# A four-layer image network on one core: VectorE takes the centered copy of the scan's first norm, and the variances' product is issued one chunk later

## The chip, the cores and the metric

The kernel runs on one core of one Trainium2 chip. The metric is the device time of one execution in microseconds (us). The engines named here are TensorE (PE in the profile; its weight loads are PEld), VectorE (DVE), ScalarE (ACT), GpSimd (POOL) and SyncE (SP), which issues most of the DMAs. TensorE writes its products to PSUM; ScalarE and VectorE read them from there.

## The reference

The input is eight images of 64 channels and 128 x 128 pixels, in fp32. Four layers follow each other, each of the form x + layer(groupnorm(x)): a deformable convolution, a 3 x 3 convolution, a pair of scans in two directions (an S5 block), and a layer of neighbours and upsampling. The change lies in the third, at the first layer norm over the 64 channels of a pixel:

```python
def _layer_norm(x, g, b):
    mu = jnp.mean(x, axis=-1, keepdims=True)
    var = jnp.mean((x - mu) ** 2, axis=-1, keepdims=True)
    return (x - mu) * jax.lax.rsqrt(var + EPS) * g + b
def _s5_block(x, i, ln1_g, ln1_b, ...):
    fx = _layer_norm(x, ln1_g[i], ln1_b[i])
    h = _s5_scan(fx, lam_re[i], lam_im[i], B_re[i], B_im[i], C_re[i], C_im[i], D[i], log_step[i])
    x = jax.nn.gelu(h) + fx
    ...
```

The x that enters here is a group-normalised one, and the mean over channels is the same for both scan directions, so the centered and scaled values are made once and used by both.

## The kernel before

Two images make a pair: 2 x 64 channels fill the 128 partitions, and a pair's 128 x 128 pixels lie along the free dimension. There are four pairs. The deformable layer runs first for all pairs (some 14,200 us); then, pair by pair, come the 3 x 3 convolution (`conv3x3`), the scans (`scan_layer`) and the last layer (`neighbours`), whose steps are partly laid into the next pair's convolution.

`scan_layer` begins with `first_norm`, which works through the 16,384 pixels of a pair in 32 chunks of 512 (`CH`), four to a block (index `n`, from the last block to the first; `m` counts the chunks in a block). For each chunk:

- L902: a product with the centering matrix, scaled by the group norm's factor, gives the centered values `pc` in PSUM. The PSUM tag "x" has two buffers, so the third centering reuses the buffer of the first.
- L904: ScalarE squares `pc` plus a bias column `cn` into `sq`. The tiles alternate between the tags "sq" and "xt", one buffer each.
- L905: ScalarE copies `pc` plus `cn` into `bf`, the room of the pair (in the profile: `room`).
- L906: `variances` (L855, the product on L858) multiplies a matrix of channel means with `sq`; the four chunks of a block write four strips of 32 partitions in one PSUM tile `pv` (in the profile: `l1v`).

After four chunks ScalarE copies `pv` to `vs` (L908, again in the buffer of tag "sq"). `by_pixel` (L860) transposes it (L865) and takes the reciprocal root on VectorE: fifteen small steps of `rsqrt` (L111 to L121). One block later `scale` (L890) spreads those roots over the channels: GpSimd copies them wide (L872), TensorE transposes them (L875), VectorE multiplies `bf` by them (L894).

`first_norm` is a generator. From its second block on, each block is followed by two steps of `back`, the backward scan of the first direction. A step of `back` holds `drive` (L1235 a product, ScalarE's copy `v` L1237, a second product L1238, two VectorE multiplications L1241 that read `pv` and `pt`, a GpSimd addition L1242), `inputs` (L1224: two ScalarE instructions that scale `bf`, each followed by two DMAs L1226 issued by SP), and `scan` (L1250 a small product, L1255 ScalarE's copy of it, L1257 two scans on VectorE, and a DMA of the result issued by SP, L1271). `inputs` reads what `scale` has multiplied, so the four L1224 of a block wait for the last L894 of that block.

The order of instructions on each engine is not the order of the source. The builder lays it out by priority (the earlier in the source, the higher) among what is ready in its own reckoning, then every engine runs its own list strictly in order, with semaphores for the dependences.

Of the kernel before, what the change touches and what calls it, by code (L numbers as in the profile page):

```python
# [11 lines left out]
AF = mybir.ActivationFunctionType  # L12
# [29 lines left out]
class Net:  # L42
# [835 lines left out]
    def first_norm(self, wp, p, a, b, r, nb):  # L878


        nc = self.nc
        af, bf = a.rearrange("p h w -> p (h w)"), b.rearrange("p h w -> p (h w)")
        center = wp.tile([P, P], F32, tag="center_r", name=f"center_r{p}", bufs=1)
        nc.vector.tensor_scalar(center, self.center, r, None, ALU.mult)
        pn = self.ps1.tile([P, 1], F32, tag="small", name=f"cn{p}")
        nc.tensor.matmul(pn, lhsT=self.center, rhs=nb, start=True, stop=True)
        cn = wp.tile([P, 1], F32, tag="cn", name=f"cns{p}", bufs=1)
        nc.vector.tensor_copy(cn, pn)

        def scale(n, y):  # L890
            for m in range(4):
                s = slice((4 * n + m) * CH, (4 * n + m + 1) * CH)
                rb = self.spread(wp, "y", y[:, 8 * m : 8 * m + 8], f"l1_{p}_{n}_{m}", ("ms0", "ms1")[m % 2])
                nc.vector.tensor_mul(bf[:, s], bf[:, s], rb)  # L894

        late = None
        for n in range(NCH // 4 - 1, -1, -1):
            pv = self.ps1.tile([P, CH], F32, tag="small", name=f"l1v{p}_{n}")
            for m in range(4):
                s = slice((4 * n + m) * CH, (4 * n + m + 1) * CH)  # L900
                pc = self.ps.tile([P, CH], F32, tag="x", name=f"pc{p}_{n}_{m}")
                nc.tensor.matmul(pc, lhsT=center, rhs=af[:, s], start=True, stop=True)  # L902
                sq = wp.tile([P, CH], F32, tag=("sq", "xt")[m % 2], name=f"sq{p}_{n}_{m}", bufs=1)
                nc.scalar.activation(sq, pc, AF.Square, bias=cn)  # L904
                nc.scalar.activation(bf[:, s], pc, AF.Identity, bias=cn)  # L905
                self.variances(pv, m, sq)  # L906
            vs = wp.tile([P, CH], F32, tag="sq", name=f"vs{p}_{n}", bufs=1)
            nc.scalar.copy(vs, pv)  # L908
            if late:
                scale(*late)  # L910
            y = self.by_pixel(vs, f"l1_{p}_{n}")
            if late:
                yield
            late = n, y
        scale(*late)
        yield
# [506 lines left out]
```

## Time and profile before

| What | Value |
|---|---|
| Timed runs of before, median | 18815.32 us (3 runs, 18770.06 to 18828.75) |
| Profiled execution, time | 18647.43 us |
| Profiled execution, span first to last instruction | 18645.6 us, mean granted TensorE clock 0.763 |
| Busy over the span | PE 11123.6, DVE 11377.5, ACT 3024.1, POOL 11000.0 us |
| L902 centering, L858 variances | 256 instructions each (two per product), median 595 and 617 ns |
| L904 square, L905 copy | 128 each, median 687 and 680 ns |
| L894 scaling | 128, median 681 ns |
| L1224 scan inputs, whole kernel | 512, mean 1292 ns |

[...] The busy time of TensorE depends on the clock it is granted, so the same instruction has short and long records. The profiled execution was 0.9% shorter than the median of the timed runs, so sums made from its rows are compared with its own span, not with the median.

In a line of the timeline stand the start and length in us, the engine, the line, the operation, the tile written and the tiles read, the count of merged instructions, and in brackets how long the engine had been idle before and who released it. In a line of waits stand the waiting instruction, the one it waited for, the us in total, the number of times and the longest. In a line of groups stand the busy us and mean ns, then the idle us ahead of the group and what ended it.

### The profile page before, as it was taken

The page shows a single profiled execution, that of the slowest core. Times are in us where ns is not written, and L with a number is a line of the kernel's source. Part 1 is how long each engine was busy: PE and PEld are TensorE (multiplying, and loading weights), DVE is VectorE, ACT ScalarE, POOL GpSimd, SP SyncE. Part 2 cuts the span into 40 slices and gives each one's busy share as a digit, 9 for nine tenths or more (in the row PEclk, how much of TensorE's full clock was granted, in tenths as well). Part 3 has the DMA queues.
Part 4 walks back from the last instruction along what each step waited for, and adds up shares of the span by engine and source line. Part 5 has one row for each costly group of instructions (what it writes and reads, how often), then busy time and mean ns, then how long its engine had stood idle before and what let it go on. Part 6 is the DMA issues. An engine that isn't in the chain of part 4 may idle for free. (4 is left out here: it accounts for less than half of the span.)

```text
span 18645.6 us, 118301 instructions
## 1 busy us (share of the span) xinstructions
PE 11123.6 (60%) x31224; PEld 3929.2 (21%) x31224; DVE 11377.5 (61%) x27180; ACT 3024.1 (16%) x5658; POOL 11000.0 (59%) x10484
## 2 busy tenths in 40 slices
PE   6655455545555554445654555555427988889886
PEld 1111111111111111111111111111102434435343
DVE  5566666556665556656665566555664765667566
ACT  1000111001100000010000000000003425334242
POOL 5766766666666666766666676766671413315142
PEclk8777677767777666777776777667658989999898
DMA  4333333333333333333333333333333243422423
GB/s 150 103 100 104 116 113 116 109 112 111 117 111 98 97 94 113 112 113 110 100 95 100 93 99 99 99 96 93 92 92 94 69 144 79 130 87 70 142 76 101
DMA packets 900049, 1933.33 MB, mean 104 GB/s; under 512 B 199852, under 2 KB 435764, under 8 KB 876340
## 3 DMA queue, kind: packets, MB, share of 16 engines
q0 software_dynamic: 442368, 1208.55, 21.7%
q1 hardware_dynamic: 381968, 679.49, 11.9%
q10 hardware_dynamic: 75044, 37.72, 1.0%
q8 instruction: 255, 4.18, 0.1%
q14 instruction: 414, 3.39, 0.1%
HBM read 1540.72 MB, written 208.10 MB: 94 GB/s over the span
## 5 line engine op out<-in xcount | busy, mean ns | idle before, releaser
L371 POOL DMA_INDIRECT g<-table,idx x9216 | 9526.3, 1034 | 4333.7 <-issue 2626.2
L381 DVE TENSOR_REDUCE sm<-g 128x64 f32<-128x256 f32 x9216 | 5062.9, 580 | 3356.0 <-remote 2479.9
L289 PE MATMUL po<-xe,wt 128*54 128x512 f32 (+3 forms) x8384 | 4668.4, 666 | 534.0 <-ACT ob L299 390.9
L380 DVE TENSOR_TENSOR g<-g,wts 128x256 f32<-128x256 f32 x9216 | 3561.8, 415 | 552.9 <-DMA g<-table,idx 488.5
L387 PE MATMUL sp<-ident,sm 128*128 128x128 f32 x4096 | 1494.5, 375 | 3632.2 <-DVE sm L381 1853.0
L390 ACT COPY s<-sp 128x512 f32<-128x512 f32 x1024 | 598.1, 584 | 9537.5 <-remote 3918.3
L387 PEld LDWEIGHTS sp<-ident,sm 128*128 128x128 f32 x4096 | 619.5, 155 | 6387.2 <-DVE sm L381 2381.4
L395 PE MATMUL yp<-s,wd 128*64 128x512 f32 (+1 forms) x2560 | 933.0, 736 | 1367.3 <-ACT s L390 756.3
L289 PEld LDWEIGHTS po<-xe,wt 128*54 128x54 f32 x8384 | 916.4, 138 | 1863.7 <-issue 1192.8
L872 POOL COPY l_yb<-ln_y 128x512 f32<-128x512 f32 x128 | 72.8, 612 | 1295.9 <-DVE ln_y L121 1295.9
L588 PE MATMUL c<-room,l_w 128*64 128x508 f32 (+1 forms) x3072 | 741.8, 597 | 22.2 <-DMA room<-nx 16.1
L1242 POOL TENSOR_TENSOR u<-u,v 128x512 f32<-128x512 f32 x256 | 327.9, 1281 | 680.0 <-DVE v L1241 548.8
L1224 ACT ACTIVATE fx<-room,ln_b,ln_g 128x512 f32<-128x512 f32 x512 | 639.2, 1292 | 169.9 <-DMA in<-fx 148.1
L1334 POOL TENSOR_TENSOR ms<-ms,ln_y 128x512 f32<-128x512 f32 x256 | 274.0, 1090 | 640.2 <-DVE ln_y L121 600.3
L389 PE MATMUL s<-ident,sm 128*64 128x128 f32 x1024 | 343.5, 335 | 449.7 <-DVE sm L381 151.2
L396 DVE BATCH_NORM_STATS2 ystat<-yp 128x6 f32<-128x512 f32 x128 | 89.3, 697 | 844.2 <-PE yp L395 498.7
L395 PEld LDWEIGHTS yp<-s,wd 128*64 128x64 f32 (+1 forms) x2560 | 222.9, 161 | 1810.2 <-issue 1000.3
L1257 DVE TENSOR_TENSOR_SCAN z<-tabs,z,u 128x256 f32<-128x256 f32 x512 | 435.4, 876 | 214.8 <-POOL u L1242 186.2
L1235 PE MATMUL pv<-in,tabs 128*128 128x512 f32 x1024 | 506.4, 617 | 41.9 <-DVE u L1241 40.0
L1320 PE MATMUL pc<-outs,h 128*128 128x256 f32 x2048 | 497.7, 386 | 28.0 <-DVE h L1305 25.8
L1302 PE MATMUL py<-x,outs 128*128 128x512 f32 x1024 | 507.3, 599 | 6.8 <-POOL x L1288 6.4
L1302 PE MATMUL py<-in,outs 128*128 128x512 f32 x1024 | 507.3, 608 | 1.7 <-ACT h L1304 1.0
(414 smaller groups left out, 10197.6 us busy)
## 6 DMA issues: line engine op xcount, KB each, us to landing
g<-table,idx POOLq DMA_INDIRECT x9216
in<-fx SPq DMA_DIRECT2D x1024, 128.0 KB
xe<-in_x_dram SPq DMA_DIRECT2D x56, 1408.0 KB
table<-q SPq DMA_DIRECT2D x256, 256.0 KB
y<-ys SPq DMA_DIRECT2D x128, 256.0 KB
room<-in_x_dram SPq DMA_DIRECT2D x64, 512.0 KB
yr<-y SPq DMA_DIRECT2D x64, 512.0 KB
room<-nx SPq DMA_DIRECT2D x256, 128.0 KB
```

What stands on the lines that cost most here:

```text
L289: nc.tensor.matmul(po[:, r0:r1, c0:c1], lhsT=wt[:, t, :], rhs=xe[:, row + r0 : row + r1, c0 + dx : c1 + dx], start=n == 0, stop=n == len(u ...
L371: nc.gpsimd.indirect_dma_start(out=tq[:, k, :], out_offset=None, in_=flat[i], in_offset=bass.IndirectOffsetOnAxis(ap=idx[:, at : at + 1], ...
L380: nc.vector.tensor_mul(t[:, k], t[:, k], w)
L381: nc.vector.tensor_reduce(sm[:, k], t[:, k].rearrange("p q c -> p c q"), axis=mybir.AxisListType.X, op=ALU.add)
L387: nc.tensor.transpose(sp[:, j, :], sm[:, j * P : (j + 1) * P], self.ident)
L390: nc.scalar.copy(st[i][:, 0:4, m * P : (m + 1) * P], sp)
L395: nc.tensor.matmul(yp[i * C : (i + 1) * C, :], lhsT=wd[0:rows, j, :], rhs=st[i][0:rows, j, :], start=j == 0, stop=j == 4)
L588: nc.tensor.matmul(o, lhsT=lt, rhs=mv, start=k < 2, stop=k >= len(calls) - 2)
L1224: nc.scalar.activation(fx[:, e].rearrange("p h (o m) -> p h o m", m=self.INNER), src[:, e::2], AF.Identity, bias=w["ln1_b"], scale=w["ln1_g"])
L1235: nc.tensor.matmul(pv, lhsT=tabs[:, at : at + P], rhs=fx[:, :, h, :], start=h == 0, stop=h == 1)
L1302: nc.tensor.matmul(py, lhsT=lt, rhs=mv, start=n == 0, stop=n == len(calls) - 1)
L1320: nc.tensor.matmul(pc[:, i], lhsT=hs[:, h, i, m * P : (m + 1) * P], rhs=self.outs[:, CEN : MIX + P], start=True, stop=True)
```

## The change

ScalarE no longer writes the centered values: VectorE does, with an addition of the same bias column out of the same PSUM tile. The variances' product of a chunk is issued after the centering, square and copy of the next chunk; the last chunk's product follows the loop. The number of instructions is the same: 128 ScalarE copies become 128 VectorE additions. No tile, buffer or DMA is added or removed.

```diff
                 nc.tensor.matmul(pc, lhsT=center, rhs=af[:, s], start=True, stop=True)
                 sq = wp.tile([P, CH], F32, tag=("sq", "xt")[m % 2], name=f"sq{p}_{n}_{m}", bufs=1)
                 nc.scalar.activation(sq, pc, AF.Square, bias=cn)
-                nc.scalar.activation(bf[:, s], pc, AF.Identity, bias=cn)
-                self.variances(pv, m, sq)
+                nc.vector.tensor_scalar_add(bf[:, s], pc, cn)
+                if m:
+                    self.variances(pv, m - 1, before)
+                before = sq
+            self.variances(pv, 3, before)
             vs = wp.tile([P, CH], F32, tag="sq", name=f"vs{p}_{n}", bufs=1)
             nc.scalar.copy(vs, pv)
             if late:
```

## The prediction

> **What bounds the kernel now.** I went from the whole to the place. By the page's 40 slices the last quarter of the span is the part after the sampling stage; the edited lines L902 to L906 run there and nowhere else: 128 chunks, 32 for each of four image pairs, in four stretches of about 145 us that begin at 14231, 15365, 16490 and 17620 us. Together they are some 575 us of 18645.6, 3.1%. I took the busy time of each engine in the first stretch, then in parts of one turn of its loop:
>
> ```profile
> 14231.00:14375.00 144.00, 123.83 (x352) 47.09 (x353) 62.48 (x176) 79.81 (x116) 28.97 (x39) 0.84 0.24 63
> ...
> 14319.98:14340.51 20.53, 17.84 (x52) 6.98 (x53) 10.03 (x28) 11.61 (x18) 4.82 (x6) 0.83 0.30 78
> 14318.31:14321.37 3.06, 0.36 (x3) 0.30 (x3) 2.70 (x8) 3.06 (x5) 0.22 (x1) 0.86 0.78 189
> 14321.37:14327.55 6.18, 6.18 (x7) 1.29 (x8) 1.99 (x9) 2.94 (x5) 2.27 (x4) 0.51 0.57 159
> 14327.55:14335.20 7.65, 7.65 (x31) 3.62 (x30) 3.08 (x5) 2.48 (x5) 1.27 (x1) 1.00 0.00 0
> ```
>
> The columns are the stretch, its length, then busy us of TensorE, its weight loads, VectorE, ScalarE, GpSimd, and the granted clock. A turn (four chunks, two scan steps) takes 20.53 us. TensorE has work for 17.84 of them, ScalarE for 11.61, VectorE for 10.03. TensorE stands nearly still for 3.06 us while ScalarE is full, and then works for 6.18 us at a clock of 0.51 before it comes back to 1.00. Its waits in that first stretch:
>
> ```profile
> PE l1v L858 <- ACT sq L904: 9.1, 7, 2.9
> PE pn L1250 <- DVE ln_t L120: 6.6, 4, 1.7
> ```
>
> The other three stretches give 9.0, 9.1, 9.0 and 6.6 each time: 36.2 and 26.4 us in all. The timeline shows what makes the square late:
>
> ```profile
> 14315.72 2.54 ACT L1224 ACTIVATE fx<-room,ln_b,ln_g 128x512 f32<-128x512 f32 x2 [0.52 <-DVE room L894]
> ...
> 14318.20 2.48 ACT L1224 ACTIVATE fx<-room,ln_b,ln_g 128x512 f32<-128x512 f32 x2
> ...
> 14319.98 0.35 PE L1250 MATMUL pn<-z,tabs 128*128 128x2 f32 x2 [1.67 <-DVE ln_t L120]
> ...
> 14320.62 0.70 ACT L904 ACTIVATE sq<-pc,cns 128x512 f32<-128x512 f32 x1
> ...
> 14321.20 0.69 ACT L905 ACTIVATE room<-pc,cns 128x512 f32<-128x512 f32 x1
> 14321.37 1.91 PE L858 MATMUL l1v<-sq,imgmean 128*32 128x512 f32 x2 [1.03 <-ACT sq L904]
> ...
> 14321.57 0.75 DVE L1257 TENSOR_TENSOR_SCAN z<-tabs,z,u 128x256 f32<-128x256 f32 x1
> ...
> 14323.21 2.08 PE L902 MATMUL pc<-room,center_r 128*128 128x512 f32 x2
> ...
> 14325.22 1.92 PE L858 MATMUL l1v<-sq,imgmean 128*32 128x512 f32 x2
> 14325.33 0.69 ACT L904 ACTIVATE sq<-pc,cns 128x512 f32<-128x512 f32 x1 [2.27 <-PE pc L902]
> ```
>
> So the loop closes thus: last multiplication of the late block (L894, ends 14315.68), four scan inputs L1224 on ScalarE (5.0 us), the first square, the variances' product, then TensorE without a gap until the next L894. The copy L905 stands behind the square: it is not in this loop. And TensorE already runs both centerings (L902, four instructions at 14316.35) before the first variances' product: the order that the second half of the edit asks for is there, although the source has it otherwise.
>
> **The change, part by part.**
>
> *ScalarE loses 128 copies.* L905 has a median of 0.680 us: 128 x 0.680 = 87 us of busy time go, 2.7 in a turn. After them ScalarE waits anyway (the third square waits 2.27 us for its product). The second square starts 0.57 us sooner (14321.20, not 14321.77), but its product comes after the third centering at 14325.22. On the path: 0.
>
> *VectorE gains 128 additions from PSUM.* This shape with this operation is not in the trace. Nearest are a copy out of PSUM with 512 columns and L1166, a scalar operation with a column of scalars out of PSUM, with 256 and 384 columns:
>
> ```profile
> L259 DVE COPY q<-tp 128x512 f32<-128x512 f32 x128 | 87.1, 680 | 12.4 <-PE tp L257 11.3 <-DMA table<-q 1.0
> ...
> L1166 DVE TENSOR_SCALAR d<-d,own 128x384 f32<-128x384 f32 x48 | 29.0, 605 | 0.0
> ...
> L1166 DVE TENSOR_SCALAR d<-d,own 128x256 f32<-128x256 f32 x16 | 7.5, 477 | 21.8 <-PE d L1163 21.8
> ```
>
> The slope of L1166 is (605 - 477) / 128 = 1.0 ns a column, so 733 ns at 512; the copy says 680. I take 0.70: 128 x 0.70 = 90 us, 2.8 in a turn, which lifts VectorE to 12.8 of 20.53. Chunks three and four fall into an idle stretch of 8.12 us (before L894 at 14331.64), which hides them. The first two fall among the scans and the small steps of the reciprocal root. That chain would end 1.4 us later, at 14325.3; GpSimd's four copies (2.27 us, now ended at 14326.0) would then end near 14327.4, and TensorE wants the first at 14330.95. Cover left: 3.5 us. Without it, each further us costs 28 us (seven closed turns in four pairs).
>
> *A new wait: the next centering for VectorE.* The third centering reuses the bank of the first, so it now waits for VectorE's copy. Are the two reads of one product side by side? The first use of pv, read by both engines, says no:
>
> ```profile
> 14266.55 0.59 ACT L1237 COPY v<-pv 128x512 f32<-128x512 f32 x1 [1.70 <-PE pv L1235]
> 14267.17 0.69 DVE L1241 TENSOR_TENSOR u<-pv,tabs 128x512 f32<-128x512 f32 x1 [9.81 <-ACT v L1237]
> ```
>
> VectorE idled 9.81 us until ScalarE's read of the same product had ended, and began 0.03 us after it. So the copy follows the square. The square ends at 14321.32, VectorE's second scan at 14322.32; copy until 14323.02 (0.70) or 14323.05 (0.73); with 0.05 us for the release the centering can start at 14323.1. It starts now at 14323.21, when TensorE is done with the slow variances' product. Cost: 0, or 0.1 us with one small step in front, 28 x 0.1 = 3 us. The upper end is a copy behind the whole reciprocal root chain (ends 14324.05): copy until 14324.75, centering at 14324.8, 1.6 us late, 28 x 1.6 = 45 us. The lower end is 0: nothing on the loop becomes shorter. I take 2 us. Behind the waiting copy stand small steps and the scale multiplications on VectorE; these have the 3.5 us above. No DMA is issued anew or moved past another.
>
> [...]
>
> *The product behind the next centering.* One product for each chunk either way, 0.85 to 1.0 us at full clock; in the first chunks of a pair, without scan steps, the trace goes by 2.03 us a chunk with TensorE unbroken (centering 14236.29, variances 14237.34, centering 14238.32). There the third centering's bank would be free at 14234.44 + 0.70 = 14235.14, before its 14236.29. Cost 0.
>
> Sum: -0 + 0 + 2 + 0 = 2 us. On the profiled execution (18647.43 us, span 18645.6) that gives 18649. That execution lies 0.9% under the median of the three timed runs, 18815.32; I carry the difference over and predict 18815, a change too small to be seen. A measurement of this kernel can tell about 0.3% from no change: faster is below 18759, slower above 18872.
>
> **Rivals.**
>
> *Faster: the order of the engines closes up.* What the builder lays out differs from the source, by when things are ready in its own reckoning, and with ScalarE lighter it could put a square before the scan inputs, or less work between the variances and the last L894. Then TensorE's waits go, 36.2 + 26.4 = 63 us (18752), and if it never stands still, the slow clock too: 6.18 x (1 - 0.51) = 3.03 us a turn, 28 x 3.03 = 85 us more (18667). Middle: 18710. For it: 2.7 us of idling in a turn are there to be had, and the clock row shows idling paid twice. Against it: all four inputs are ready when the first starts and are earlier in the source, and the edit touches none of them.
>
> [...]
>
> *Slower: VectorE holds the bank.* The additions stand behind the reciprocal root's steps in VectorE's order, the third centering comes 1.6 us late, and TensorE idles inside the stretch in which its clock should recover. Restarting the 6.18 us after the slow product of 1.84 us adds 1.84 x 0.49 = 0.9 us. Per turn 2.5, x 28 = 70 us: 18885. It decides as soon as the copy ends 0.15 us after 14323.05, and is past what can be told from 2.0 us a turn on. For it: the scans and the small steps fill 2.70 of 3.06 us just there. Against it: now the scans already slip in between these steps.
>
> *The edit does not do what it says*: reads follow each other, the order was there. That is part of my forecast, at the same time.
>
> **How the numbers follow.** No visible change 0.43: its working has bounds of 0 and 45 us, both inside 0.3%. Faster 0.28, slower 0.29: the order is laid out anew by a reckoning I cannot follow, and 2 us a turn suffice either way. Range 18690 to 18905: it holds the first case, most of the slower one and of the faster one down to three quarters of the way from 18759 to 18667; about 0.2 is left out.
>
> **What would show it.** Right: turns of about 20.5 us; L858 still waits some 36 us for squares; VectorE's additions of 0.68 to 0.73 us start as the squares end; ScalarE's busy time lower by 87 us. Wrong: L902 waiting for the new additions by over 1 us a turn and a longer slow-clock stretch (slower), or no wait of L858 and a clock near 1.00 in the stretches (faster). A squaring ahead of the scan inputs in ScalarE's order would make the prediction wrong at once.

## The result and the profile after

Twelve timed runs of the changed kernel have a median of 18818.11 us (18730.65 to 18856.55), twelve of the kernel before 18799.76 us (18726.26 to 18830.86). The ratio on record is 1.0004 with a 95% interval of 0.9989 to 1.0019 (the quotient of the two medians is 1.0010): no difference that can be measured, as forecast. The 2 us that the forecast's sum came to are far below what these runs can tell. The profiled execution has a span of 18780.6 us, 135 more than before's, but 124 of these lie ahead of the first norm (its first product starts at 14355.4, not 14231.2 us), in code that the change doesn't touch. So all that follows goes by the trace of the part concerned: the *four stretches* from L886, the first product of the first norm, to the first output product of the scan (L1302; lines after L905 are three higher in the changed kernel). They take 183.2, 174.6, 179.9 and 179.8 us before, in sum 717.5, and 179.3, 179.2, 184.0 and 179.4 us after, in sum 721.9: 4.4 us more.

The view of one line, for the new additions on VectorE in the kernel after:

```profile
L905 DVE TENSOR_SCALAR room<-pc,cns x128: 743/750/752, 14358.6 to 17886.6; 128x512 f32<-128x512 f32 x128
its engine sat idle before it (us, times) until:
  ACT sq L904: 106.7, 69
who waited for it (us, times):
  PEld pc L902: 12.9, 16
```

128 additions with a median of 0.750 us, and the idle times ahead of 69 of them ended with a square. Next the busy times of a settled turn (from a block's first variances' product, L858, to the next block's) and its parts, after, with the columns as in the prediction:

```profile
14442.47:14462.91 20.44, 16.71 (x53) 7.37 (x53) 13.62 (x32) 9.41 (x14) 4.86 (x6) 0.83 0.30 79
14438.75:14442.47 3.72, 0.00 (x1) 0.00 (x1) 2.49 (x7) 3.72 (x6) 0.93 (x1) 0.83 0.73 168
14442.47:14448.48 6.01, 6.01 (x11) 2.17 (x12) 3.01 (x10) 1.37 (x3) 2.27 (x4) 0.54 0.44 117
14448.48:14455.82 7.34, 7.34 (x33) 3.73 (x32) 4.82 (x8) 2.21 (x4) 1.28 (x1) 1.00 0.00 0
```

The turn is 20.44 us (20.53 before). ScalarE works 9.41 us in it (11.61 before), VectorE 13.62 (10.03). TensorE now stands still in one piece, for 3.72 us, and then works for 6.01 us at a granted clock of 0.54. The waits of TensorE in the first 146 us of the first stretch of the kernel after:

```profile
PE l1v L858 <- ACT sq L904: 23.0, 7, 5.1
PE cn L886 <- DVE gn_nb L149: 3.3, 1, 3.3
PE l_rb L875 <- DVE room L894: 0.4, 1, 0.4
```

The wait ahead of the small product (L1250 before, L1253 after) is gone from this list and the wait for squares has grown from 9.1 to 23.0 us (91.8 over the four stretches). The timeline of the kernel after shows why:

```profile
14436.88 4.91 ACT L1227 ACTIVATE fx<-room,ln_b,ln_g 128x512 f32<-128x512 f32 x4 [1.25 <-DVE room L894]
...
14441.68 0.15 ACT L1258 COPY z<-pn 128x2 f32<-128x2 f32 x1
14441.72 1.27 ACT L904 ACTIVATE sq<-pc,cns 128x512 f32<-128x512 f32 x2
...
14442.47 2.49 PE L858 MATMUL l1v<-sq,imgmean 128*32 128x512 f32 x4 [3.72 <-ACT sq L904]
```

The four scan inputs (L1227, L1224 before) still stand ahead of the squares, in one piece now, and the two squares follow each other without the copy between. TensorE makes both variances' products there before the third centering; before, it made one.

### The profile page after: what moved, and what is told of

It reads as the page before. It is cut to its first block, busy times and chain, and to the rows that moved or that the text cites. A ratio compares the mean times of both kernels' runs of the same rounds, so it can differ in the third digit from the quotient of the medians.

```text
span 18780.6 us, 118357 instructions
## 1 busy us (share of the span) xinstructions
PE 11000.9 (59%) x31224; PEld 3926.2 (21%) x31224; DVE 11460.3 (61%) x27308; ACT 2952.7 (16%) x5530; POOL 11065.3 (59%) x10484
## 5 line engine op out<-in xcount | busy, mean ns | idle before, releaser
L289 PE MATMUL po<-xe,wt 128*54 128x512 f32 (+3 forms) x8384 | 4593.3, 657 | 504.9 <-ACT ob L299 283.0
L588 PE MATMUL c<-room,l_w 128*64 128x508 f32 (+1 forms) x3072 | 739.3, 596 | 21.6 <-DMA room<-nx 15.2
L1227 ACT ACTIVATE fx<-room,ln_b,ln_g 128x512 f32<-128x512 f32 x512 | 638.9, 1291 | 200.2 <-DMA in<-fx 147.4
```

Of the source, the lines that this page charges most:

```text
L289: nc.tensor.matmul(po[:, r0:r1, c0:c1], lhsT=wt[:, t, :], rhs=xe[:, row + r0 : row + r1, c0 + dx : c1 + dx], start=n == 0, stop=n == len(u ...
L588: nc.tensor.matmul(o, lhsT=lt, rhs=mv, start=k < 2, stop=k >= len(calls) - 2)
L1227: nc.scalar.activation(fx[:, e].rearrange("p h (o m) -> p h o m", m=self.INNER), src[:, e::2], AF.Identity, bias=w["ln1_b"], scale=w["ln1_g"])
```

## The experiments

The runs were made on several chips (the record names 10, 12 and 13). The sampling stage doesn't take equally long in all runs (the first norm starts near 12,030 us in some and near 14,100 to 14,360 in others, both among those on chip 12), the part behind it hardly differs (e6 and e12, one program: 644.6 and 639.0 us over the four stretches), so the kernels are compared by their four stretches. "Turns" are from one copy L908 to the next, in the settled part of a stretch.

| Kernel | Four stretches, us | Sum |
|---|---|---|
| before | 183.2, 174.6, 179.9, 179.8 | 717.5 |
| before again (e13) | 182.0, 178.8, 173.8, 173.5 | 708.1 |
| after | 179.3, 179.2, 184.0, 179.4 | 721.9 |
| e1, VectorE's copy alone | 179.4, 179.3, 178.8, 175.6 | 713.1 |
| e2, new order alone | 183.4, 184.1, 183.6, 183.4 | 734.5 |
| e3, two squares on GpSimd | 172.0, 167.2, 171.2, 171.0 | 681.4 |
| e4, additions twice | 185.2, 186.5, 186.0, 184.8 | 742.5 |
| e5, inputs split, on after | 166.2, 167.3, 168.0, 168.0 | 669.5 |
| e6, inputs split, on before | 159.3, 162.9, 159.5, 162.9 | 644.6 |
| e8, e3 and e5 together | 164.5, 167.6, 162.6, 162.0 | 656.7 |
| e9, three useless products | 179.4, 179.6, 179.5, 179.6 | 718.1 |
| e10, two useless products | 171.5, 171.8, 173.1, 173.0 | 689.4 |
| e11, inputs split, on e2 | 164.6, 165.4, 164.9, 164.9 | 659.8 |
| e12, e6 timed | 159.3, 159.6, 160.9, 159.2 | 639.0 |

**The halves alone.** e1 takes only VectorE's copy:

```diff
-                nc.scalar.activation(bf[:, s], pc, AF.Identity, bias=cn)
+                nc.vector.tensor_scalar_add(bf[:, s], pc, cn)
                 self.variances(pv, m, sq)
```

> The kernel before with the first half of the change alone: VectorE writes the centered copy, the variances' product stays where it was in the source. Measure: the four stretches from the first-norm's first product to the first output product of the scan, summed (717.5 us before, 721.9 us with the whole change). Theory (the turn is closed by scan inputs, square, variances on ScalarE and TensorE; the copy is not in it): 712 to 728 us, a turn of 20.3 to 20.6 us. Rival (two parts that cancel: the copy gains or loses, the order gives it back): this stretch sum moves by over 15 us in one direction, and by as much the other way with the order alone.

e2 takes only the later product:

```diff
                 nc.scalar.activation(bf[:, s], pc, AF.Identity, bias=cn)
-                self.variances(pv, m, sq)
+                if m:
+                    self.variances(pv, m - 1, before)
+                before = sq
+            self.variances(pv, 3, before)
```

> The second half of the change alone: ScalarE still copies, the variances' product follows the next chunk's centering in the source. Theory: 712 to 728 us for the four stretches, and TensorE's order of centerings and variances in a settled turn as before. Rival (two parts that cancel): over 15 us away from 717.5, on the other side than the copy alone.

e1 gave 713.1 us, with the same waits as the whole change (23.0 us for squares in its first stretch), and in a settled turn every engine has the instructions of the changed kernel in the same order: what the change does to the settled turn comes from the copy. e2 gave 734.5 us, outside what the theory allowed and on the rival's side. Its settled turn has before's order and before's waits (over the first 160 us of the stretches 9.0 us for squares against 9.1, and 10.1 for the small product in both); all its settled turns are 20.5 us.

To see what 17 us mean here, e13 ran the kernel before once more, unchanged.

> The kernel before once more, unchanged, to see how far its four stretches move from one execution to the next (717.5 us in the first profile, of which one stretch 174.6 and one 183.2; 734.5 us with the new product order alone, whose order of instructions in a settled turn is the same). If the phase of the clock at a stretch's start decides: single stretches again spread over 174 to 184 us, and the sum is anywhere from 700 to 735 us. If the new order costs the 17 us itself: 714 to 721 us.

708.1 us, as the first of the two cases allowed and below the 714 to 721 of the second: eight stretches of one and the same program lie between 173.5 and 183.2 us. Two stretches of before show where that comes from. Here are the busy times of one turn of the same instructions in each, first in the stretch that took 183.2 us, then in the one that took 174.6:

```profile
14321.37:14341.89 20.52, 17.84 (x52) 6.98 (x52) 10.03 (x28) 11.60 (x18) 4.82 (x6) 0.83 0.30 78
```

```profile
15451.66:15469.38 17.72, 15.03 (x53) 6.57 (x53) 10.04 (x28) 11.61 (x18) 4.82 (x6) 1.00 0.34 89
```

And the two waits of TensorE ahead of that second turn, from its timeline:

```profile
15450.26 0.35 PE L1250 MATMUL pn<-z,tabs 128*128 128x2 f32 x2 [1.66 <-DVE ln_t L120]
15451.66 1.05 PE L858 MATMUL l1v<-sq,imgmean 128*32 128x512 f32 x2 [1.04 <-ACT sq L904]
```

The pauses are the same to 0.02 us, 1.66 and 1.04 us, and all engines have the same instructions in the same order. In one the clock is granted in full, the products take 1.05 us instead of 1.9, TensorE is busy for 15.03 us, and the turn is 2.8 us shorter. So single stretches move by up to ten us without any change. That e2's four stretches all take over 183 us, while only one of before's eight does, stays unexplained: its first blocks are laid out a little differently, and they may decide in which of the two ways a stretch goes on. It isn't shown that the order itself costs nothing.

The comparison of turns at full clock shows something that the sums hide. In its fourth stretch e1 has turns at a clock of 1.00, with the order of the changed kernel:

```profile
15481.31:15499.31 18.00, 14.29 (x53) 6.56 (x53) 13.62 (x31) 9.38 (x14) 4.86 (x6) 1.00 0.34 88
```

So with the copy on VectorE a turn at full clock takes 18.00 us, against 17.72 before: TensorE is busy for 0.74 us less (15.03 to 14.29) and stands still for 1.0 us more. At the slow clock the two are as good as alike (20.44 and 20.52). So the change costs 0.28 us a turn at full clock, and the slow clock hides it.

**Doubling the suspected cost.** e4 makes each addition twice, with the same result.

```diff
                 nc.vector.tensor_scalar_add(bf[:, s], pc, cn)
+                nc.vector.tensor_scalar_add(bf[:, s], pc, cn)
```

> The changed kernel with each VectorE addition done twice, 128 more instructions of 0.75 us (96 us of VectorE). Theory (VectorE has room beside the loop; only the first two copies of a block can touch it, through the bank that the third centering needs): the four stretches grow by 0 to 45 us, to 722 to 767 us, and what grows is TensorE's wait at the centering for the additions. Rival (VectorE's added work is on the path in full and was only paid back by what ScalarE lost): plus 80 to 96 us, 800 us or more.

742.5 us: 96 us more work on VectorE cost 20.6. VectorE has room, as the theory has it, and the rival's 80 to 96 us are out. But the theory's place was wrong: TensorE does not wait for the additions (0.2 us at L902 in the first 140 us). Its waits moved: there are 7.3 us ahead of the small product, behind VectorE's scans, where after had none, and 15.5 us for squares instead of 23.0. Over the whole first stretch TensorE stands still for 38 us in both kernels and is busy for 147.0 us instead of 141.0, so what exactly makes the 20.6 us stays open.

**Taking the square out of ScalarE's queue.** e3 makes the squares of the first two chunks of a block on GpSimd, from the copy.

```diff
-                nc.scalar.activation(sq, pc, AF.Square, bias=cn)
+                if m > 1:
+                    nc.scalar.activation(sq, pc, AF.Square, bias=cn)
                 nc.vector.tensor_scalar_add(bf[:, s], pc, cn)
+                if m < 2:
+                    nc.gpsimd.tensor_mul(sq, bf[:, s], bf[:, s])
```

> The changed kernel with the squares of the first two chunks of each block made by GpSimd from the centered copy, so that they don't stand behind the scan inputs on ScalarE. Theory (the loop is closed through ScalarE's queue): TensorE's wait for squares (23 us a stretch) falls below 10 us, the turn from 20.4 to 16.5 to 19 us, the four stretches by 40 to 110 us to 612 to 682 us. Rival (TensorE's own rate is the bound, the wait only shows where its slack is): the turn stays above 20 us, the stretches above 705 us.

681.4 us, 40.5 less than after, at the upper edge of what was expected; waits for ScalarE's squares fell to 3.9 us up to the last centering of the first stretch, turns from the third on to 16.3 to 18.8 us, at clocks of 0.87 to 1.00. The loop goes through ScalarE's queue.

**Shortening what stands ahead of the square.** e5 makes one of the two scan inputs of a step on VectorE, in the backward scan beside the first norm; e6 does it on the kernel before.

```diff
-            nc.scalar.activation(fx[:, e].rearrange(...), src[:, e::2], AF.Identity, bias=w["ln1_b"], scale=w["ln1_g"])
+            to = fx[:, e].rearrange(...)
+            if e and f and not self.d:
+                nc.vector.tensor_scalar(to, src[:, e::2], w["ln1_g"], w["ln1_b"], ALU.mult, ALU.add)
+            else:
+                nc.scalar.activation(to, src[:, e::2], AF.Identity, bias=w["ln1_b"], scale=w["ln1_g"])
```

> The changed kernel with one of the two scan inputs of each step, in the backward scan beside the first norm, made by VectorE instead of ScalarE, which halves what stands ahead of the square. Theory A (the loop through ScalarE sets the turn us for us): the turn falls from 20.45 by about 2.5 us to 18 us, at a granted clock near 0.83 as now; four stretches 645 to 665 us (721.9 with the change). Theory B (as long as TensorE pauses long enough, the granted clock halves for part of the turn and holds the turn at 20.48 us; with a short pause both go): the turn falls to 16.3 to 17.7 us with the clock at 0.95 to 1.00; four stretches 600 to 645 us. Rival (TensorE's own rate): over 705 us.

> The kernel before with the same split of the scan inputs. The theory that the change left the loop as it was says the same as of the changed kernel with the split, within 15 us over the four stretches; if the change had taken anything away or put anything in that another limit hid, the two differ by more.

e5: settled turns of 17.57 us at a clock of 1.00, as theory B has it; the sum, 669.5, is over both ranges, because the second and third turn of a stretch (15.2 to 16.8 and 18.7 to 20.4 us) together gained next to nothing (35.4 to 37.1 us, 35.6 in three stretches of after). e6: 644.6 us, turns of 18.3, 15.6, 19.4 and 14.6 us in alternation, mean 17.0, all at 1.00. The two differ by 25 us, more than the 15 that the theory allowed. With the loop relaxed, the change costs something that had been hidden, as in e1's turns at full clock. e11 asked which half of it:

> The split of the scan inputs on the kernel that has the new order of the variances' product but ScalarE's copies. The split gave 644.6 us over the four stretches on the kernel before and 669.5 on the changed one. If VectorE's copies are what costs the 25 us there: 640 to 652 us here. If the order does: 662 to 675 us.

659.8 us lies between the two answers. Its settled turns are those of e6 to 0.1 us (18.27, 15.57, 19.34, 14.61), with a mean of 16.95, those of e5 are 17.57; so in the settled turns it is VectorE's copies that cost some 0.6 us a turn. The rest of the difference lies in the first turns: e11's second turns take 16.3 us at a clock of 0.90, those of e6 12.6 us at 1.00 in two stretches and 15.3 at 0.78 in the other two. The split in us between the two halves stays open.

e8 joins e3 and e5.

> The changed kernel with both: squares of the first two chunks by GpSimd, and half of the scan inputs by VectorE. Theory A and B alike: below the better of the two alone (681.4 us with the squares), 590 to 670 us, turn 16 to 17.5 us at a clock of 1.00. Rival (VectorE, now with copies and inputs, becomes the bound: about 12.8 + 2.7 us of a turn): a turn no shorter than with the squares alone, and TensorE waits for VectorE.

656.7 us: better than either, in the range, and worse than e6, which leaves the copies on ScalarE. But the turns expected were 16 to 17.5 us, and there are settled ones from 15.1 to 21.6, with a mean of 18.1 that is no better than e3's 17.9; the gain lies in the turns ahead of them. That is in part what the rival said: VectorE is busy for 109.86 us of the first 141, and TensorE's longest wait is for VectorE's scans (11.5 us in the first stretch).

**More work in the pause.** If slow clock and pause belong together, filling the pause with useless work should shorten the turn. e9 repeats centering products, with the same result.

```diff
-                nc.tensor.matmul(pc, lhsT=center, rhs=af[:, s], start=True, stop=True)
+                for _ in range((2 + m) if late and m < 2 else 1):
+                    nc.tensor.matmul(pc, lhsT=center, rhs=af[:, s], start=True, stop=True)
```

> The changed kernel with useless work: beside the backward scan the centering product of the first chunk of a block is made twice and that of the second three times, with the same result, so that TensorE has three more products (about 3 us at full clock) where it pauses for the square. Theory A: the turn stays at 20.4 us or grows a little, clock 0.83. Theory B: the pause is short, the clock stays up, and the turn falls to 17 to 19 us although TensorE does more; four stretches 630 to 700 us. Rival (TensorE's own rate): the turn grows by 2.5 to 3 us to about 23, four stretches 780 us or more.

One turn of e9:

```profile
14266.00:14285.70 19.70, 18.89 (x58) 7.57 (x58) 12.85 (x32) 9.42 (x14) 4.82 (x6) 1.00 0.30 80
```

The clock is 1.00 in every turn, and the turn is 0.74 us shorter than after's although TensorE makes three products more. 18.89 of 19.70 us are busy now, so there is little left to fill; that would account for a turn that fell less than theory B expected (17 to 19 us) and for a sum, 718.1, over the 630 to 700. Against e1's turn of 18.00 us at full clock, with the same work but for the repeats, the three products cost 1.7 us. Theory A (same turn, clock 0.83) and the rival (23 us) are out. With two repeats (`for _ in range(3 if late and m == 1 else 1)`):

> The changed kernel with two useless products a block instead of three (the second chunk's centering made three times, same result). If the clock is what the pause costs: clock 1.00 in the settled turns, TensorE about 1 us a turn less busy than with three, a turn near 18.7 us (19.7 with three, 20.45 with none), four stretches 690 to 710 us. If the loop through ScalarE sets the turn and the clock is only a by-product: 20.4 us. If TensorE's own work sets it: above 22 us.

689.4 us, 0.6 under the range: 32.5 us less than after, with more work than after, and turns from 16.2 to 22.1 us at clocks of 0.85 to 1.00, so that the clock is not 1.00 throughout as expected. In e9 and e10 the repeats also moved other instructions in TensorE's order (in the turn of e9 a step's first product comes ahead of the second chunk's variances), so not all of it need be the clock's.

**The split of the inputs, timed.** e12 is the program of e6:

> The split of the scan inputs on the kernel before, timed. Its four stretches were 73 us shorter than before's in one look, the span from the first norm on 64 us. Theory (that time is on the path, since nothing later waits for less): ratio 0.9966, between 0.994 and 0.999. Rival (given back in the later scans): ratio 0.999 to 1.001.

Median 16372.11 us (16365.34 to 16373.09, 5 runs) against 16449.87 us (16441.77 to 16462.71, 9 runs) for the kernel before on the same chip: ratio 0.9952, interval 0.9939 to 0.9966, a gain of half a per cent. The 78 us agree with what the four stretches lost (717.5, or 708.1 in e13, to 639.0), and no sign is left of time given back later. The changed kernel was not timed beside these; by its stretches (721.9) it lies with the kernel before. Where its time lies, over the first 160 us:

```profile
12024.00:12184.00 160.00, 137.86 (x421) 56.34 (x422) 95.82 (x234) 79.14 (x123) 40.64 (x48) 0.94 0.31 81
```

TensorE is busy for 137.86 of 160 us at a mean clock of 0.94.

## Why the prediction was right, point by point

- *The loop.* The step that carried the forecast, that ScalarE's copy is not in the loop and its four scan inputs are, holds: e3 and e6 shortened the stretches by 40 and 73 us by touching the square and the inputs, while the copy, alone or with the order, moved their sum (713.1 and 721.9) by no more than an unchanged program moves by itself (708.1 and 717.5). "On the path: 0" holds for the slow turns alone: at full clock the turn with VectorE's copy is 0.28 us longer (18.00 and 17.72).
- *The order.* "The order that the second half of the edit asks for is there" held for the kernel before. It did not hold after: with the copy gone from ScalarE the builder put the second variances' product ahead of the third centering, the opposite of what the edit asks for. e1 has the same waits without the order's half.
- *The wait of L858.* The step that failed: some 36 us of waiting for squares were to stay. There were 91.8 us. The 26.4 us of waits for the small product moved there, and the pause of a turn grew from 2.69 to 3.72 us. The turn stayed, because TensorE's busy time fell from 17.84 to 16.71 us. Of these 1.13 us, 0.74 are there at full clock too (15.03 and 14.29), where products that belong together follow each other directly (at a clock of 1.00 four instructions of L858 take 1.62 us in after, at 14404.09, and two take 1.05 before); the other 0.39 are less time lost to the slow clock (2.81 and 2.42). The sum was right for a reason that I had not seen: in that the turn came out the same, it was luck.
- *The price of the addition.* 0.70 us taken, 0.733 the upper bound by the slope of L1166, 0.750 measured; 96 us in place of 90, and none of it to be seen in the slow turn.
- *Side by side.* Where VectorE is free, the copy starts with the end of the square, as the case of `pv` said. At 14427.11 the third square of a block starts and lasts 0.69 us; the addition starts at 14427.83, 0.03 us after its end. Taken in order, each of the 128 additions starts after its square has ended, by 0.03 us at the least and 1.8 at most; whether the two could read at once is not shown.
- *The bank.* Bounded between 0 and 45 us, taken as 2. The 45 rest on a root chain that ends at 14324.05; its last step starts at 14323.34 and lasts 0.19, so it ends at 14323.53, and the same working gives 1.1 us a turn, some 30 us. The weight loads of L902 waited 12.9 us for the additions, in part behind running products; the products of L902 themselves are in none of the four stretches in the list of TensorE's waits. The term was right in size.
- *ScalarE's relief.* 87 us were to go from its busy time; 3024.1 fell to 2952.7, by 71. Square and copy had overlapped (starts 0.58 us apart, 0.69 long), and busy time counts an overlap once.
- *The rivals.* Faster needed the order to close up; it opened instead. Slower needed the centering to wait for the additions; the second variances' product took that place, so that the bank was free in time. That a pause inside the slow stretch would start it over, 0.9 us a turn, was an estimate from the row of 6.18 us; no run put a pause there alone. The price of the slow clock, 3.03 us a turn by the granted clock, is 2.81 by the turns of before at both clocks (20.53 and 17.72, busy 17.84 and 15.03). The part of *slower* that is real is 0.28 us a turn at full clock, some 8 us over 28 turns, and the timed runs can't show it.

## What to carry to other kernels

Relieving an engine that is busy for half of a turn was worth nothing here, because the instructions taken away do not stand in the loop that sets the turn; follow the queue ahead of the instruction waited for (here four scan inputs), and shorten that. Where instructions are laid out by a builder, moving one from an engine to another moves the others too: compare the order, not the edit. And before a few us are explained, see how far an unchanged kernel moves: here a stretch has two ways of running that differ by 2.8 us a turn, and a cost of 0.28 us a turn shows only in one of them.

## What the runs showed of the hardware

- The same instructions with the same pauses ran at a granted clock of 1.00 or 0.83 in different stretches of one execution, with turns of 17.72 and 20.52 us. After pauses of 1.66 and 1.04 us TensorE worked at half clock (0.51) for 6.18 us or not at all.
- Where the clock changes is in the traces too. In those of before and after it is granted at 1.00 or 0.50, and each of the 118 stays inside the eight stretches lasts 3.41 us or a whole multiple of it (up to ten times). Here is before's slow turn, cut where the clock changes (columns as in the prediction):

```profile
14320.53:14327.36 6.83, 5.99 (x7) 1.16 (x8) 2.60 (x10) 3.79 (x8) 2.27 (x4) 0.50 0.58 162
14327.36:14341.01 13.65, 11.85 (x46) 5.82 (x45) 7.38 (x18) 7.78 (x10) 2.54 (x2) 1.00 0.15 36
14341.01:14347.84 6.83, 5.95 (x7) 1.12 (x8) 2.66 (x10) 3.81 (x8) 2.27 (x4) 0.50 0.57 160
```

- The two ways in which a stretch goes on differ in how the pause lies to these changes. Here are the pieces of 3.41 us, cut along the stays, that hold the longer pause of before's slow turn and of its fast one:

```profile
14317.12:14320.53 3.41, 1.55 (x5) 0.49 (x3) 2.23 (x9) 3.41 (x4) 1.28 (x1) 1.00 0.61 142
15446.93:15450.35 3.42, 1.76 (x5) 0.50 (x4) 2.32 (x7) 3.42 (x5) 1.27 (x1) 1.00 0.49 113
```

  TensorE is busy for 1.55 us of the first, and the clock halves at its end; it is busy for 1.76 us of the second, and the clock stays. Such pieces of before and after, from 9 us after a stretch's start on, were counted: of those at full clock, all 43 in which TensorE was busy for less than 40% were followed by half clock, none of the 202 over 60%, and 16 of the 28 between; of those at half clock, all 57 under 80% were followed by half clock again, 49 of the 50 over 95% by full clock, and 10 of the 13 between. No run varied the busy share of a piece by itself.
- With three useless products in the pause (e9) the clock stayed at 1.00, and the turn became shorter (20.44 to 19.70 us).
- The settled slow turns are remarkably alike: 20.5 to 20.6 us before, 20.4 to 20.5 in e13 and e2, 20.3 to 20.7 after, though the pause differs by 1.0 us. In before and after the stays of the settled slow turns are two pieces at half clock and four at full, turn after turn (6.83 and 13.65 us), so that the half clock comes back every 20.48 us. The turns run in step with it there, which fits that turns of 17.72 and 18.00 us at full clock can hardly be told apart at the slow one. What keeps them in step is not shown by a run that varies it, and e4's settled turns take 20.75 to 22.75 us, at clocks of 0.85 to 0.92.
- The kernel before takes 16450 us in the nine runs beside e12 and 18800 us in the twelve beside after: the difference lies in the sampling stage (first norm at some 12,030 or 14,200 us in runs of either kind), where GpSimd's 9216 indirect DMA instructions take 958 ns each in e12 and 1036 ns in e6, the same program, and GpSimd idles ahead of them for 2824 and 4152 us. What makes the difference is not shown; the record names chip 12 for e6 and e12 alike.
